# Own-part products of a four-layer graph kernel: six of them made among layer 2's sums, the rest within layer 1

## The chip, the cores and the metric

The kernel runs on one core of one Trainium2 chip. The metric is the device time of one execution in microseconds (us): the median of five runs before the change is 1888.71 us (1886.83 to 1902.47). A change of less than about 0.5% (9.4 us) is about what a measurement of this kernel can't tell from no change.

## What is computed

Four graph layers run one after the other over 3327 nodes with 512 features. Layers 0 and 3 are attention layers; layer 1 takes the mean over all neighbours; layer 2 takes the mean over the first 64 neighbours. Each layer adds its result to its input and normalises the rows. Layer 2 is the one whose parts move, and layer 1 stands just before it:

```
# layer 1
agg = mask @ x / max(deg, 1)
out = relu(concat(x @ W_self + b_self, agg @ W_nb + b_nb) @ W_comb + b_comb)
x = layernorm(x + out)
# layer 2
nb_mean = sum of the first 64 neighbours' rows / max(count, 1)
xj = leaky_relu(nb_mean @ W_nb.T + b_nb)
xi = leaky_relu(x @ W_line.T + b_line)      # the own part
x = layernorm(x + xi + where(count > 0, xj, 0))
```

The own part xi needs a block's rows of x alone and no neighbour. The weights W_nb and W_line have to be transposed on the chip first.

## The kernel before

**Tiling.** The 3327 rows are 26 blocks of 128 (the last has 127). `xres[b]` holds block b's rows in the chip's memory from layer to layer. Each block has a list of its neighbours, cut into chunks of 128 edges; block 0 is dense and takes 26 chunks of whole table rows instead, blocks 1 to 25 have 19 chunks (block 1) down to 5, 201 in all. In layers 1 and 2 a chunk's neighbour rows are gathered from a table in DRAM (`t1_d`, `t2_d`; 1024 fp32 numbers a row, so 512 KB a chunk) by an indirect DMA of POOL (L973), and summed into the block's accumulator by two matmuls with a 0/1 selection matrix `selr` (L1491).

**Ring.** The gathered chunks lie in a ring of buffers (class `Ring`, L576): in layers 1 and 2 one part of 11 slots (`gm`) and one of 4 (`gn`), by the constants `RING` (L544) and `MORE` (L545). A gather waits until the matmuls that read its slot's last content are done. `groups` (L953) cuts a list into groups of at most 4 chunks and never across the end of a part; `first_items` (L1445) gives block 0's chunks in groups of 4, and `take` (L588) skips a part with less room than the group.

**Order of the work.** From L1438 on the order of the instructions is the order in which the code emits them. Generators stand in two lists, `work` and `ends`; `both` (L1499) advances each by one `yield`. `mean_group` (L1460) is a group: gather, selection, matmuls, one step each (layer 2 before has one step more: DVE writes the selection as 8-bit numbers into `sall`, L1476, which layer 3 reads again, and ACT then turns it into `selr`, L1483). When a block's last group is summed, `layer1_end` (L1531) or `layer2_end` (L1640) follows, a step at a time, between the next groups' instructions.

**Layer 1.** `layer1_end` normalises the block, transposes it (four small matmuls, L751, and an ACT copy, L754), multiplies it by W_nb (`wn2`, L1545, four matmuls at L766), adds the bias (DVE, L1548), splits it into two parts (`halves`: an ACT cast at L822, a DVE subtraction at L824) in a tile `t2` with one buffer, and SP stores that to the table `t2_d` (L739). Then block 0's layer-2 sum is made from the same tile (L1561). `self_part` (L1522) makes layer 1's own part for the last 16 blocks with the weights `wx`, one per group, in the first 16 groups.

**Layer 2's own parts.** `own_part` (L1570) multiplies a transposed block by W_line (`wl2`, L1576) and three DVE instructions (L1579 to L1581) add the result to `xres[b]`. For b < 26 - `LATE` = 16 it is started inside `layer1_end` with the transposed block at hand (L1550). The blocks 16 to 25 are put on the list `late`; the loop at L1595 starts them one per step once layer 1's groups are all emitted, each with transposes of its own:

```
        while late or work.live or ends.live:
            if late and not work.live:
                ends.add(own_part(late.pop(0)))
            both()
```

Layer 2's groups are emitted after this loop, so on PE all ten late own parts stand ahead of layer 2's first matmul.

**Layer 2 needs all of layer 1.** Its first gather on POOL waits until the last `t2` has landed in `t2_d`. The blocks come in the order of `mixed` (L1450): 1, 25, 24, 23, 22, 2, 21, 20, 19, 18, 3 and so on; block 1 is big, the blocks from 15 on have 5 or 6 chunks. `score_parts` (L1613) prepares layer 3's weights at the start of layer 2.

**Weights.** `transposed_weights` (L1406) loads and transposes both W_nb and W_line near the end of layer 0, through one buffer.

**After layer 2** POOL clears the ring for layer 3 (L1670, two memsets: 11616 and 4096 columns), `finish` (L1021) makes a few table-wide numbers, and layer 3 begins: its ring has 22 slots and 3 (of 520 columns), and four further pieces of the same 4096 columns hold the rows of its dense block 0 (`first_block`, L1099).

Of the kernel before, what the change touches and what calls it, by code (L numbers as in the profile page):

```python
# [536 lines left out]
LATE = 10  # L537
# [7 lines left out]
MORE = 4096  # L545
# [77 lines left out]
def sparse_path(ctx, tc, flag_i, x, adj, l0_w, l0_a1, l0_a2, l1_w_self, l1_b_self, l1_w_nb, l1_b_nb,  # L623
# [366 lines left out]
    class Gat:  # L990
# [108 lines left out]
        def first_block(self, pool, ps, pacc, mp, none, done, room):  # L1099
# [4 lines left out]
            for h in range(H):  # L1104
# [10 lines left out]
            held = [t.rearrange("p (h m) -> p h m", m=M) for t in  # L1115
                    (room[:, q * H * M:(q + 1) * H * M] for q in range(GROUP))]
            G = held[-1]
# [7 lines left out]
            def unit(c):  # L1125
                m = LAST if c == NB - 1 else P
                G = held[c % GROUP]
# [139 lines left out]
    wx = pool_in(wxlay, "l1wx", side="right").tile([P, DC, D], F32, name="wx")  # L1267
# [138 lines left out]
    def transposed_weights():  # L1406

        for src, o in ((l2_w_nb, wn2), (l2_w_line, wl2)):
            for k in range(DC):
                raw = fin.tile([P, D], F32, name="raw", tag="tb")  # L1410
                nc.sync.dma_start(raw, src[k * P:(k + 1) * P, :])
                yield
                yield
                pt = ps.tile([P, DC, P], F32, name="pt", tag="tr")
                for c in range(DC):
                    nc.tensor.transpose(pt[:, c, :], raw[:, c * P:(c + 1) * P], ident)
                nc.scalar.copy(o[:, :, k * P:(k + 1) * P], pt)

    w2lay = ExitStack()
    for k, item in enumerate(groups(pools[0], order)):  # L1420
# [5 lines left out]
        if ready == NB - 1 and wn2 is None:  # L1426
            listlay.close()
            aside = pool_in(ctx, "s_more")
            sp = pool_in(ctx, "s_sel", 3)
            wp = pool_in(w2lay, "l2w")  # L1430
            wn2 = wp.tile([P, DC, D], F32, name="wn2")
            wl2 = wp.tile([P, DC, D], F32, name="wl2")
            work.add(transposed_weights())
# [26 lines left out]
    def mean_group(item, table, whole0, done, sall=None):  # L1460
# [11 lines left out]
        else:  # L1472
            G = gather(ring, table, l, c0, g)
            yield
            if sall is not None:
                have = select(sp, l.dst, c0, g, BF16, kept(sall, b, at, g))  # L1476
                yield
            S = sp.tile([P, GROUP, P], F32R, name="selr")
            if sall is None:
                nc.vector.tensor_tensor(S[:, :g], lane1[:, None, :].to_broadcast([P, g, P]),  # L1480
                                        l.dst[:, c0:c0 + g, None].to_broadcast([P, g, P]), ALU.is_equal)
            else:
                nc.scalar.activation(S[:, :g], have, AF.Identity)  # L1483
# [18 lines left out]

    ring = Ring(2 * D, room.tile([P, RING], F32R, name="gm", tag="ring").bitcast(F32),
# [3 lines left out]
    left0 = [0]  # L1507


    with ExitStack() as lay:  # L1510
# [5 lines left out]
        nc.sync.dma_start(bl, row(l2_b_line, D))  # L1516
        ps = pool_in(lay, "l1ps", 2, space=PSUM)
        xts = pool_in(lay, "l1xt", 3)
        acc0 = pool_in(lay, "l1p0", space=PSUM).tile([P, D], F32, name="acc0")
        early, late = list(range(NB - LATE0, NB)), []  # L1520
# [10 lines left out]
        def layer1_end(b, acc):  # L1531
# [38 lines left out]
        def own_part(b, xt=None):  # L1570

            yield
            if xt is None:
                xt = transposed(xts, ps, xres[b])
                yield
            po = times(ps, xt, wl2)  # L1576
            yield
            xi = fin.tile([P, D], F32, name="xi")
            nc.vector.tensor_add(xi, po, bl)  # L1579
            nc.vector.scalar_tensor_tensor(xi, xi, SAGE_ALPHA, xi, ALU.mult, ALU.max)  # L1580
            nc.vector.tensor_add(xres[b], xi, xres[b])  # L1581

        for items in (first_items(), groups(ring, range(1, NB))):
            for item in items:
# [15 lines left out]
    wxlay.close()  # L1600
# [3 lines left out]
    with ExitStack() as lay:  # L1604
        fin = pool_in(lay, "l2f", 2)
        ps4 = pool_in(lay, "l2p4", 4, space=PSUM)
        ps = Banks(pool_in(lay, "l2p2", 2, space=PSUM), po=ps4)

        wp = pool_in(lay, "l3w")
# [30 lines left out]
        def layer2_end(b, acc):  # L1640
            yield
            y = xres[0]
# [16 lines left out]
        for item in groups(ring, mixed()):  # L1659
            work.add(mean_group(item, t2_d, None, lambda b, acc: ends.add(layer2_end(b, acc)), sall))  # L1660
# [10 lines left out]
        g3.finish(fin, ps)  # L1671
    mlay.close()


    with ExitStack() as lay:
        pools = (Ring(H3 * (OUT3 + 2), rows, extra[:, :MORE - GROUP * H3 * (OUT3 + 2)]), pool_in(lay, "l3s", 3),
# [13 lines left out]
        def verdict():  # L1690
# [11 lines left out]
            for ls in lists:  # L1702
                for l in ls:
# [16 lines left out]
                               nl, layer3, extra[:, MORE - GROUP * H3 * (OUT3 + 2):])  # L1720
# [61 lines left out]
```

## Time and profile before

| | |
|---|---|
| median of 5 runs | 1888.71 us (1886.83, 1886.95, 1888.71, 1896.29, 1902.47) |
| the profiled execution | 1884.82 us, its span 1882.9 us |
| mean granted TensorE clock | 0.914 |
| layer 1's sums (first to last matmul of L1491) | 717.9 to 1104.1 us |
| layer 2's sums | 1172.0 to 1458.0 us |
| layer 3's first sums of block 0 | from 1498.7 us |
| PE, DVE, ACT, POOL busy | 82%, 65%, 42%, 48% of the span |

How to read it: PE does the matmuls, DVE and ACT work on tiles, POOL issues the gathers, SP the plain loads and stores. A line of the timeline has a start, a duration, an engine, a line of the kernel, what it writes <- reads and, in brackets, how long the engine was idle before and what ended that. A line of the table by stretch has for each engine its busy time and (x) its instructions, then the granted clock of PE, the busy share of the 16 DMA engines and what they moved in GB/s. At a DMA share of about 1.00 or a little above the DMA engines have no free time.

### The profile page before, as it was taken

Reading aid. Unit: us, or ns where it says so; the run is one execution under the profiler, and the core shown is the slowest. Engines: PE = TensorE matmul, PEld = TensorE weight load, DVE = VectorE, ACT = ScalarE, POOL = GpSimd, SP = SyncE. Lnnn points to the kernel's source line nnn. Section 1 sums busy time; section 2 is a strip of 40 time slices with the busy share of each in tenths; the row PEclk is TensorE's granted clock in tenths of the full one; section 3 lists DMA queues with packets and bytes.
Section 4 is the critical chain, followed back from the end, with each engine's and each line's share of the span. In section 5 each row is a group of like instructions: output and inputs, shape, how many; then the busy total and the mean of one; then the engine's idle time right before and its main releaser. Section 6 shows DMA issues by size and latency. Waiting matters only on the chain.

```text
span 1882.9 us, 24596 instructions
## 1 busy us (share of the span) xinstructions
PE 1541.0 (82%) x7493; PEld 1052.8 (56%) x7493; DVE 1228.2 (65%) x3217; ACT 783.7 (42%) x2465; POOL 900.2 (48%) x984
## 2 busy tenths in 40 slices
PE   5898767888999998998899987769777657877775
PEld 4665545665666664554455543457556445656654
DVE  7999857787887862134677764534344566766786
ACT  5557834555755753210111121234233212545564
POOL 1000265455655522546656613766665433666660
PEclk9899879999999999999899999798898778998897
DMA  8624776776766538999999944999999264666661
GB/s 293 207 82 135 265 223 205 239 242 199 256 213 195 175 107 320 369 332 388 360 365 379 377 152 180 342 362 338 373 370 335 93 194 116 190 192 189 194 191 47
DMA packets 146178, 460.50 MB, mean 245 GB/s; under 512 B 24357, under 2 KB 25893, under 8 KB 146038
## 3 DMA queue, kind: packets, MB, share of 16 engines
q0 software_dynamic: 93776, 329.72, 53.2%
q1 hardware_dynamic: 52262, 129.14, 19.5%
q8 instruction: 61, 1.00, 0.2%
q14 instruction: 79, 0.65, 0.1%
HBM read 403.93 MB, written 54.85 MB: 244 GB/s over the span
## 4 chain that ended last, share of the span: by engine, by line
PE 48%; DVE 19%; issue 10%; DMA 8%; ACT 6%; another core or an unknown queue 5%; POOL 3%; SPq 1%; DVEq 0%; ACTq 0%; POOLq 0%
PE po L766 16%; PE acc L1205 14%; PE acc L1491 7%; PE po L1005 5%; DMA gm<-t_d,idx 4%; DVE cand L884 3%; PE pt L751 2%; POOL gm L973 2%; PE pg L1177 1%; DVE cand L898 1%; DVE sl L896 1%; DMA gx<-t_d 1%; DVE gr L1197 1%; DVE gt L1197 1%
## 5 line engine op out<-in xcount | busy, mean ns | idle before, releaser
L973 POOL DMA_INDIRECT gt<-t_d,idx x243 | 239.5, 986 | 394.6 <-DVE some L900 216.3
L973 POOL DMA_INDIRECT gm<-t_d,idx x300 | 302.1, 1007 | 229.6 <-PE acc L1491 65.6
L1205 PE MATMUL acc<-gt,sel 128*128 128x264 f32 (+2 forms) x972 | 245.0, 399 | 1.9 <-issue 1.9
L973 POOL DMA_INDIRECT gr<-t_d,idx x177 | 170.7, 965 | 153.4 <-issue 47.5
L1205 PE MATMUL acc<-gr,sel 128*128 128x260 f32 (+2 forms) x708 | 195.9, 427 | 34.0 <-issue 27.4
L766 PE MATMUL po<-wn,xt 128*128 128x512 f32 x416 | 205.5, 640 | 14.9 <-ACT xt L754 7.1
L1491 PE MATMUL acc<-gm,selr 128*128 128x512 f32 (+3 forms) x636 | 197.5, 442 | 21.3 <-DMA gm<-t_d,idx 13.2
L1205 PEld LDWEIGHTS acc<-gt,sel 128*128 128x128 f32 (+2 forms) x972 | 182.8, 195 | 51.6 <-issue 24.9
L1205 PEld LDWEIGHTS acc<-gr,sel 128*128 128x128 f32 (+2 forms) x708 | 142.3, 209 | 68.1 <-issue 38.9
L1491 PEld LDWEIGHTS acc<-gm,selr 128*128 128x128 f32 (+3 forms) x636 | 117.0, 196 | 73.6 <-DMA gm<-t_d,idx 24.1
L1005 PE MATMUL po<-w,xt 128*128 128x262 f32 x416 | 115.7, 439 | 46.5 <-issue 29.4
L1197 DVE TENSOR_TENSOR gt<-gt,pg 128x1536 f32<-128x1536 f32 (+3 forms) x75 | 140.6, 1875 | 16.0 <-ACT sel L1192 13.8
L766 PEld LDWEIGHTS po<-wn,xt 128*128 128x128 f32 x416 | 81.7, 204 | 108.6 <-issue 89.9
L1005 PEld LDWEIGHTS po<-w,xt 128*128 128x128 f32 x416 | 89.0, 219 | 73.0 <-issue 34.9
L973 POOL DMA_INDIRECT gn<-t_d,idx x102 | 102.6, 1006 | 54.7 <-issue 22.1
L884 DVE MAX8 cand<-val 128x8 f32<-128x832 uint16 (+38 forms) x259 | 125.4, 524 | 0.0
L751 PE MATMUL pt<-s_ident,xres 128*128 128x128 f32 x520 | 83.0, 285 | 43.0 <-DMA xres<-in_x_dram 18.0
L1005 PE MATMUL po<-gt,xt 128*128 128x268 f32 x416 | 107.9, 405 | 2.6 <-ACT xt L758 1.3
L1165 ACT ACTIVATE far<-place,nmid 128x384 int16<-128x384 int16 (+3 forms) x139 | 87.8, 634 | 49.4 <-issue 25.2
L751 PEld LDWEIGHTS pt<-s_ident,xres 128*128 128x128 f32 x520 | 64.4, 146 | 72.5 <-issue 44.4
L754 ACT COPY xt<-pt 128x512 f32<-128x512 f32 x86 | 50.6, 588 | 128.6 <-PE pt L751 70.1
L1197 DVE TENSOR_TENSOR gr<-gr,pg 128x1536 f32<-128x1536 f32 (+3 forms) x56 | 101.8, 1817 | 2.7 <-ACT gr L1190 2.3
(283 smaller groups left out, 2848.3 us busy)
## 6 DMA issues: line engine op xcount, KB each, us to landing
t_d<-t SPq DMA_DIRECT2D x50, 512.0 KB
ab<-in_adj_dram SPq DMA_DIRECT2D x25, 832.0 KB
ab<-in_adj_dram SPq DMA_DIRECT2D x25, 831.5 KB
gm<-t_d POOLq DMA_DIRECT2D x17, 512.0 KB
t_d<-tg SPq DMA_DIRECT2D x25, 264.0 KB
t_d<-tg SPq DMA_DIRECT2D x25, 260.0 KB
gx<-t_d SPq DMA_DIRECT2D x25, 260.0 KB
xres<-in_x_dram SPq DMA_DIRECT2D x25, 256.0 KB
```

What stands on the lines that cost most here:

```text
L751: nc.tensor.transpose(pt[:, c, :], src[:, c * P:(c + 1) * P], ident)
L754: nc.scalar.copy(xt, pt)
L766: nc.tensor.matmul(po, xt[:, c, :], w[:, c], start=c == 0, stop=c == DC - 1)
L884: nc.vector.max(out=top, in_=seg)
L896: nc.vector.max(out=top, in_=cf)
L898: nc.vector.match_replace(out=cf, in_to_replace=top, in_values=cf, imm_value=0.0)
L973: nc.gpsimd.indirect_dma_start(out=t[:m, c, :], out_offset=None, in_=table[:, :], in_offset=bass.IndirectOffsetOnAxis(ap=l.idx[:m, c0 + c: ...
L1005: nc.tensor.matmul(pw[s], xt[:, c, :], self.w[:, c, s, :], start=c == 0, stop=c == DC - 1)
L1165: nc.scalar.activation(far[:, :g * P], place[:, c0 * P:(c0 + g) * P], AF.Abs, bias=l.nmid, scale=2.0)
L1197: nc.vector.tensor_mul(Gc[:, :, :OUT], Gc[:, :, :OUT], w[:, :g].rearrange("p c (h o) -> p (c h) o", o=1).to_broadcast([P, g * H, OUT]))
L1205: nc.tensor.matmul(accs[b][s], S[:m, c, :], G[:m, c, s * hh * M:(s + 1) * hh * M], start=at + c == 0, stop=at + c == chunks_of[b] - 1)
L1491: nc.tensor.matmul(accs[b], S[:m, c, :], G[:m, c, k * D:(k + 1) * D].bitcast(F32R), start=at + c + k == 0, stop=k == 1 and at + c == n - 1)
```

## The change

- The six blocks `LATER` = 1, 2, 3, 23, 24, 25 get their own part in layer 2: it is started together with the block's first group. All other blocks get it inside `layer1_end`, if `wl2` exists by then, and at the end of layer 1 otherwise (that is block 0 alone).
- W_line is loaded and transposed in layer 1, after the last `self_part`, into the room of `wx`, which is no longer needed then. Layer 0 transposes W_nb alone, through two buffers.
- `t2` gets two buffers in layer 1 (one before), the transposed blocks four (three before).
- The ring's second part shrinks from 4096 to 2600 columns: 2 slots in layers 1 and 2 (4 before), 5 slots in layer 3 (3 before). Layer 3's dense block gets four tiles `gd` of its own.
- In layer 2 DVE writes the selection straight into `selr`, and ACT copies it to `sall` behind it; `mean_group` has one step less there, and `selr` two buffers (three before).
- `tg`, the tile that layer 2 stores for layer 3, has one buffer (two before).

The instruction streams that come of it: layer 1 has 73 groups for blocks 1 to 25 (63 before), layer 2 has 76 (65), layer 3 has 62 (64). Up to layer 1's last sum 18 own parts are made (16 before), of blocks 4 to 21.

```diff
-LATE = 10
+LATER = (1, 2, 3, 23, 24, 25)
-MORE = 4096
+MORE = 5 * 520
...
-            tb = pool.tile([P, H, self.M], F32, name="tg")
+            tb = pool.tile([P, H, self.M], F32, name="tg", bufs=2 - self.k)
...
+            S = sp.tile([P, GROUP, P], F32R, name="selr")
+            nc.vector.tensor_tensor(S[:, :g], lane1[:, None, :].to_broadcast([P, g, P]),
+                                    l.dst[:, c0:c0 + g, None].to_broadcast([P, g, P]), ALU.is_equal)
             if sall is not None:
-                have = select(sp, l.dst, c0, g, BF16, kept(sall, b, at, g))
-                yield
-            S = sp.tile([P, GROUP, P], F32R, name="selr")
-            if sall is None:
-                nc.vector.tensor_tensor(S[:, :g], ..., ALU.is_equal)
-            else:
-                nc.scalar.activation(S[:, :g], have, AF.Identity)
+                nc.scalar.activation(kept(sall, b, at, g), S[:, :g].bitcast(F32), AF.Identity, saturate=False)
...
-            t2 = fin.tile([P, 2, D], F32R, name="t2", bufs=1)
-            if b < NB - LATE:
-                ends.add(own_part(b, xt))
+            t2 = fin.tile([P, 2, D], F32R, name="t2")
+            if b in LATER or wl2 is None:
+                late.append(b)
             else:
-                late.append(b)
+                ends.add(own_part(b, fin, xts, bl, xt))
...
                 if early:
-                    ends.add(self_part(early.pop(0)))
+                    parts.append(self_part(early.pop(0)))
+                    ends.add(parts[-1])
+                elif wl2 is None and not any(map(parts.__contains__, ends.live)):
+                    wl2 = wxroom.tile([P, DC, D], F32, name="wl2", tag="wx")
+                    ends.add(transposed_weights(l2_w_line, wl2, wp))
                 both()
-        while late or work.live or ends.live:
-            if late and not work.live:
-                ends.add(own_part(late.pop(0)))
+        now = [b for b in late if b not in LATER]
+        while now or work.live or ends.live:
+            if now and not work.live:
+                ends.add(own_part(now.pop(0), fin, xts, bl))
             both()
...
         for item in groups(ring, mixed()):
+            if item[4] == 0 and item[0] in LATER:
+                ends.add(own_part(item[0], fin, fin, bias1))
             work.add(mean_group(item, t2_d, None, lambda b, acc: ends.add(layer2_end(b, acc)), sall))
```

More of the change, by code (lines that the diff above doesn't have):

```diff
@@ L1404, in sparse_path, with transposed_weights @@
     wn2 = None
[L1406 to L1411, printed above, removed]
-                yield
[L1413 to L1417, printed above, removed]
+    def transposed_weights(src, o, pool):
+        for k in range(DC):
+            raw = pool.tile([P, D], F32, name="raw")
+            nc.sync.dma_start(raw, src[k * P:(k + 1) * P, :])
+            yield
+            yield
+            pt = ps.tile([P, DC, P], F32, name="pt", tag="tr")
+            for c in range(DC):
+                nc.tensor.transpose(pt[:, c, :], raw[:, c * P:(c + 1) * P], ident)
+            nc.scalar.copy(o[:, :, k * P:(k + 1) * P], pt)
     w2lay = ExitStack()
@@ L1501, in both, with own_part @@
         ends.step()
+    def own_part(b, fin, xts, bl, xt=None):
+        yield
+        if xt is None:
+            xt = transposed(xts, ps, xres[b])
+            yield
+        po = times(ps, xt, wl2)
+        yield
+        xi = fin.tile([P, D], F32, name="xi", bufs=1)
+        nc.vector.tensor_add(xi, po, bl)
+        nc.vector.scalar_tensor_tensor(xi, xi, SAGE_ALPHA, xi, ALU.mult, ALU.max)
+        nc.vector.tensor_add(xres[b], xi, xres[b])
+        owned.add(b)
     ring = Ring(2 * D, room.tile([P, RING], F32R, name="gm", tag="ring").bitcast(F32),
```

48 lines of the change are left out of this document (17 added, 31 removed).

## The prediction

> **What bounds the kernel now.** I read the table by stretch first, for the busy share of the DMA engines from layer 1 to layer 2 (its last columns are granted clock, DMA share, GB/s):
>
> ```profile
> core 0: us, PE busy (x) PEld busy (x) DVE busy (x) ACT busy (x) POOL busy (x), PEclk, DMA share, GB/s
> 800.00:820.00 20.00, 20.00 (x66) 10.77 (x65) 5.48 (x9) 4.07 (x9) 10.40 (x12) 1.00 1.03 393
> 820.00:840.00 20.00, 20.00 (x65) 10.82 (x64) 4.80 (x11) 2.90 (x6) 9.64 (x10) 1.00 0.88 322
> 1040.00:1060.00 20.00, 20.00 (x63) 10.73 (x63) 15.09 (x33) 3.21 (x8) 11.67 (x12) 1.00 1.01 366
> 1100.00:1105.00 5.00, 5.00 (x21) 3.26 (x21) 3.94 (x7) 1.40 (x4) 0.00 (x0) 1.00 0.01 4
> ...
> 1145.00:1150.00 5.00, 3.59 (x13) 1.68 (x11) 2.08 (x3) 0.58 (x1) 3.78 (x5) 1.00 1.03 413
> 1155.00:1160.00 5.00, 4.27 (x11) 1.86 (x9) 1.19 (x2) 0.58 (x1) 0.00 (x0) 0.70 0.00 1
> 1160.00:1165.00 5.00, 4.27 (x13) 2.07 (x14) 2.21 (x4) 0.58 (x1) 0.00 (x0) 1.00 0.00 0
> 1165.00:1170.00 5.00, 3.47 (x8) 1.21 (x7) 2.17 (x5) 0.00 (x0) 0.00 (x0) 1.00 0.00 0
> 1170.00:1175.00 5.00, 3.03 (x7) 2.45 (x8) 5.00 (x16) 2.23 (x5) 1.54 (x1) 0.66 0.00 0
> 1325.00:1350.00 25.00, 18.53 (x77) 14.91 (x78) 7.31 (x20) 8.67 (x41) 15.92 (x16) 0.86 1.02 364
> ```
>
> In both layers' sums the DMA engines are full (1.01 to 1.03); in layer 1 PE is full beside them (20.00 of 20), in layer 2 it has a quarter free (18.53 of 25). Between the layers DMA stands still twice: about 1100, while layer 1's last blocks are finished, and from 1155 to 1175. POOL's timeline tells why:
>
> ```profile
> 1089.54 1.38 POOL L973 DMA_INDIRECT gm<-t_d,idx  x1 [0.30 <-PE acc L1491]
> 1132.48 0.97 POOL L973 DMA_INDIRECT gm<-t_d,idx  x1 [41.57 <-DMA t_d<-t]
> ...
> 1149.56 0.94 POOL L973 DMA_INDIRECT gm<-t_d,idx  x1 [0.30 <-issue]
> 1173.46 3.04 POOL L973 DMA_INDIRECT gm<-t_d,idx  x1 [22.95 <-PE acc L1491]
> ```
>
> Layer 2's gathers start when the last t2 has landed (1132.48), fill the ring by 1150, and then wait 22.95 us for PE to free a slot. PE's timeline shows what it does meanwhile:
>
> ```profile
> 1094.51 6.37 PE L766 MATMUL po<-wn,xt 128*128 128x512 f32 x8 [3.37 <-ACT xt L754]
> ...
> 1118.51 3.60 PE L766 MATMUL po<-wn,xt 128*128 128x512 f32 x8
> 1121.94 3.60 PE L766 MATMUL po<-wl,xt 128*128 128x512 f32 x8
> ...
> 1164.77 3.70 PE L766 MATMUL po<-wl,xt 128*128 128x512 f32 x8 [0.73 <-ACT xt L754]
> 1171.97 5.37 PE L1491 MATMUL acc<-gm,selr 128*128 128x512 f32 x16 [3.50 <-ACT selr L1483]
> ```
>
> Up to 1168.5 PE makes late own parts (po<-wl), though gathered chunks have been there since about 1140. The chain that ended last runs through them from 1118 to 1170. What the change is worth is the DMA time lost there, not PE time saved.
>
> **The parts, one by one.**
>
> 1. *The standstill from 1155 to 1175.* Layer 2's sums ran from the first gather at 1132.5 to the last matmul at 1457.3, 324.8 us, with four stretches of 5 us at share 0.00. If gathers never pause, they need 305 us from the landing of the last t2 on. **-20.**
>
> 2. *Two buffers for t2.* ACT's timeline has, at the end of layer 1:
>
> ```profile
> 1093.35 0.62 ACT L822 CAST t<-tb 128x512 fp32r<-128x512 f32 x1 [7.36 <-DMA t_d<-t]
> ...
> 1126.07 0.59 ACT L754 COPY xt<-pt 128x512 f32<-128x512 f32 x1 [6.51 <-PE pt L751]
> 1126.55 0.62 ACT L822 CAST t<-tb 128x512 fp32r<-128x512 f32 x1
> ```
>
> The cast waited 7.36 us for the last store; the copy xt behind it on ACT waited too, and PE behind that: 3.37 us idle, then a product of 6.37 us instead of 3.70 at a granted clock of 0.51. With a second buffer the cast waits for the store before. 3.37 + 2.67 = **-6**. The other such waits (55.3 us in 9 over layer 1) lie where DMA is full: nothing.
>
> 3. *The last cast.* At 1126.55 it stood behind the copy xt of a late own part, whose transposes stood behind another own product; its input (L1548) was ready at 1122.8. In the new order only block 0's own part is there, and its copy comes before. 3.7 us, and some 0.4 us more on DVE behind L1579 to L1581: **-4**.
>
> 4. *One own product more before the last products of W_nb.* In the new PE order an own product stands ahead of block 24's product too: 3.5 us, of which 1.15 us were idle (1109.72, waiting for ACT). **+2.3.**
>
> 5. *Layer 1's sums.* Blocks 0 to 3 lose their own products (4 x 3.43 = 13.7 us of PE), W_line's 16 transposes come in (4 x 0.60 = 2.4). They lie at about 820 to 920, where DMA is full but for 820 to 860 (0.88 and 0.91): -4 to 0, taken -2. Blocks 16 to 21 get own products: 6 x 3.43 = 20.6 us of PE from about 1050 to the last sum, where PE is 92 to 100% busy. A block of 6 chunks then has some 3.2 us of sums, 0.9 of small matmuls and 6.2 to 6.9 of products, 10.3 to 11 us, against 3.8 MB of DMA, about 10 us at 375 GB/s. So +0.7 each, +4; if PE was the whole bound there, 20.6 less the 5 us that it idled: +15. Taken +7. W_line's four loads of 256 KB move with it; on SP each waits for the transposes of the one before, with stores of t2 and loads of zb queued behind; zb is loaded 3 blocks ahead, so this is hidden unless a load waits longer than a block (10 us). Sum **+5** (-4 to +15).
>
> 6. *A smaller ring in layer 1.* Block 0's groups of four don't fit the part of 2 slots, so 8 slots serve them instead of 12: four chunks (2.1 MB, 5.6 us of DMA) are issued later at the start. Against that PE gets there sooner by a wait for W_line (1.76 us at 731.5) and four sets of transposes. -5 to +6, **0**.
>
> 7. *Six own parts in layer 2.* PE: 6 x (0.60 + 3.70) = 25.8 us, all within the first 92 of 201 chunks. Those take DMA some 92 x 1.5 = 138 us, in which PE was 80% busy: now nearly full. ACT 6 x 0.58, DVE 6 x 2.1 us (DVE at 40%). Hidden if the ring stays ahead; uncovered it is the whole 26. Each `layer2_end` of the six waits for its own part, which is 3 steps old by then. 0 to +26, **+4**: the first groups, where `score_parts` fills DVE too (1180 to 1190: 9.55 of 10 us), are the tight place.
>
> 8. *The selection.* DVE writes selr itself (551 ns in layer 1, L1480) where sall (545, L985) and then selr (538, L1483) stood in line; the sums wait for DMA anyway. Two buffers instead of three let DVE wait for the sums two groups back: -2 to +5, **0**. `tg` with one buffer holds ACT if a store takes over a block's 7 us or more: 0 to +3, **0**.
>
> 9. *The memset.* After layer 2 a DVE instruction of usually 547 ns (L827) takes 11.03 us beside POOL's two memsets, on the chain that ended last:
>
> ```profile
> 1458.16 9.78 POOL L1670 MEMSET gr<- 128x11616 f32 x1 [6.61 <-PE acc L1491]
> 1467.88 3.52 POOL L1670 MEMSET gx<- 128x4096 f32 x1
> ```
>
> ```profile
> 1460.66 11.03 DVE xres L827
> ```
>
> It ends as the second memset does (1471.7 and 1471.4), so the second counts. It shrinks to 2600 columns: 3.52 x 1496/4096 = **-1.3**. The Trainium skill's page "SBUF — State Buffer", section "SBUF: two separate sides", has DVE and GpSimd share one port pair as a lock held for a whole instruction. By that rule DVE could get in between the memsets and part 9 would be 0; the row shows it got in behind both. The same section warns that DVE's 2-port instructions keep GpSimd from writing its DMA descriptors, which speaks against more DVE work beside layer 2's gathers; its section "Who interferes with whom" names copies and tensor_scalar as holders of both ports, and an instruction of two tensors in SBUF only against what GpSimd reads; by it the own parts (L1579 to L1581) cost the gathers nothing.
>
> 10. *Layer 3.* 62 groups instead of 64, 27 ring slots instead of 25: -2 to +2, **0**.
>
> Sum: -20 - 6 - 4 + 2.3 + 5 + 4 - 1.3 = **-20**. The profiled execution, 1884.82 us, becomes 1865. It lies 3.9 us under the median of the five runs; against that median I predict **1869 us**. All low ends together give -42 (1847), all high ends +28 (1917).
>
> **The rivals.**
>
> *PE becomes the bound of layer 2's first half.* The hole closes, but part 7 costs 22 instead of 4: 1869 + 18 = 1887, no change. For it: PE comes to about 100% in those 138 us. Against it: its clock there was 0.80 to 1.00 after waits and rises with fewer of them.
>
> *The smaller ring starves DMA* (slower). Place: layer 2's sums. If the 15 slots and not the DMA engines set the pace, a slot turns round in 15 x 1.48 = 22.2 us (gathers came every 1.48 us from 1250 to 1460), and 13 slots give 1.71 us: 201 x 0.23 = +46. 1869 + 46 = 1915. It decides from the point where a turn-round stays above 13 x 1.48 = 19.2 us. For it: POOL's longer idle times end on freed slots. Against it: the share of 1.00 to 1.02, and only some 17 of 100 us that POOL waits beyond its usual 0.3.
>
> *The hole only moves.* Layer 2's first selections stand on DVE behind the rest of layer 1, and `score_parts` takes some 25 us of DVE; if PE's first sums come more than 18 us after the first gather, the ring is full again and DMA stops for 10 us: 1879.
>
> **How the numbers follow.** The forecast (1850 to 1877, most of the low ends, with part 7 up to 12) 0.62; the hole moves 0.10; PE the bound 0.15; the ring starves DMA 0.13. The range reaches from 1850 to 1895 and leaves out the starved ring, the high ends all at once, and the last 3 us of the low ones. Faster by over 0.5% (below 1879.3): 0.62 and half of 0.10, 0.67; within 0.5%, which is about what a measurement of this kernel can tell from no change: 0.05 + 0.15 = 0.20; slower (above 1898.1) 0.13.
>
> **What would show it.** Right: no stretch of 5 us with DMA share 0.00 after layer 2's first gather, POOL's 22.95 us gone, layer 2's last sum some 305 to 310 us after the first gather, which starts near 1128; no cast waiting for a store of t2; L827 after the last sum near 9.7 us. Wrong: a DMA share under 0.95 in layer 2's sums (the ring), PE full there with POOL waiting (PE), layer 1's last sum after 1110 (part 5).

## The result, and the profile after

The changed kernel takes 1889.59 us (median of 36 runs, 1872.43 to 1900.28) beside 1888.50 us of the kernel before (62 runs): ratio 1.0004, 95% interval 0.999 to 1.0018. The forecast gain of 20 us did not come; nothing measurable changed. The profiled execution takes 1887.61 us, its span 1885.9.

By stage, in us, from POOL's and PE's timelines (layer 1: its first gather to its last sum; tail: to layer 2's first gather; layer 2: its first gather to its last sum; middle: to layer 3's first sum of block 0):

| | layer 1 | tail | layer 2 | middle | layer 3 |
|---|---|---|---|---|---|
| before | 391.0 | 28.4 | 325.6 | 40.6 | 384.2 |
| after | 398.8 | 25.8 | 322.9 | 38.6 | 388.3 |

Layer 2, which was to lose 16 us, lost 2.7. The table by stretch of the changed kernel, with the stretches shown of before and those in which DMA now stands still (last columns: granted clock, DMA share, GB/s):

```profile
720.00:730.00 10.00, 7.56 (x21) 3.27 (x21) 1.39 (x2) 2.81 (x5) 1.19 (x3) 1.00 0.90 310
730.00:740.00 10.00, 4.59 (x11) 2.98 (x10) 0.69 (x1) 2.22 (x4) 1.27 (x3) 0.83 0.59 146
...
1060.00:1080.00 20.00, 20.00 (x65) 10.93 (x64) 15.03 (x33) 3.43 (x8) 10.65 (x11) 1.00 0.93 347
1100.00:1105.00 5.00, 5.00 (x16) 2.82 (x16) 4.72 (x13) 0.49 (x2) 0.00 (x0) 1.00 0.45 128
...
1160.00:1165.00 5.00, 0.00 (x0) 0.00 (x0) 0.00 (x0) 0.00 (x0) 2.33 (x4) 0.50 1.04 307
...
1195.00:1200.00 5.00, 5.00 (x18) 2.75 (x17) 1.53 (x3) 0.18 (x2) 0.86 (x1) 0.77 0.06 25
1200.00:1205.00 5.00, 5.00 (x25) 4.29 (x24) 4.61 (x12) 2.81 (x18) 1.08 (x1) 1.00 0.48 131
1205.00:1210.00 5.00, 5.00 (x28) 4.25 (x27) 0.36 (x1) 1.58 (x6) 0.95 (x1) 1.00 0.00 0
...
1325.00:1350.00 25.00, 19.84 (x69) 15.24 (x70) 9.93 (x26) 8.81 (x37) 15.79 (x17) 0.80 1.02 373
```

The standstill of 1155 to 1175 is gone: there the share is 0.99 to 1.04. Added up over stretches of 5 us it had cost 24 us of DMA time from 1150 to 1185. From 1195 to 1230 a new one costs 18, most of it (16) in four stretches in which PE is full (5.00 of 5: the three shown and the one from 1220). POOL's timeline has the same in its waits:

```profile
1136.04 0.97 POOL L973 DMA_INDIRECT gn<-t_d,idx  x1 [38.48 <-DMA bias<-in_L_gnn_b_line_dram]
...
1199.10 0.86 POOL L973 DMA_INDIRECT gn<-t_d,idx  x1 [7.57 <-PE acc L1482]
```

The wait of 22.95 us has gone; three of 7 us (from 1190.6 on) stand in its place, each for PE to free a slot. What PE does there:

```profile
1142.31 1.19 PE L1482 MATMUL acc<-gn,selr 128*128 128x512 f32 x2 [8.45 <-DMA gn<-t_d,idx]
...
1179.45 5.78 PE L766 MATMUL po<-wl,xt 128*128 128x512 f32 x8 [0.83 <-issue]
...
1192.06 6.30 PE L766 MATMUL po<-wl,xt 128*128 128x512 f32 x8 [4.28 <-ACT xt L754]
...
1200.47 7.23 PE L1005 MATMUL po<-w,xt 128*128 128x262 f32 x32
...
1209.81 3.60 PE L766 MATMUL po<-wl,xt 128*128 128x512 f32 x8
...
1217.67 5.49 PE L1005 MATMUL po<-w,xt 128*128 128x262 f32 x16 [3.33 <-ACT xt L760]
```

The first sums come at 1142 and not at 1172. Then the own products (po<-wl) meet the layer-3 products of the blocks that end early (po<-w), two of the own products at a mean granted clock of 0.63 and 0.58: 5.78 and 6.30 us for what takes 3.60 at 1209.81 (1.00 there). Ahead of the first PE had stood still for 7.34 us (to 1166.38), and the clock was still 0.50 up to 1180; ahead of the second for 4.28 us. The Trainium skill's page "TensorE: Matmul & The Clock Gate", section "HAM oscillation — how this bites in real kernels", warns of just this, half the clock after a pause of some 3.4 us; the 4.28 us ahead of the 6.30 agree.

ACT's timeline at three places: layer 1's first selection, the last cast of layer 1, and the stretch of the new standstill:

```profile
735.89 0.63 ACT L1466 ACTIVATE selr<-row 128x512 fp32r<-128x512 fp8e4 x1 [4.10 <-DMA t_d<-t]
...
1130.53 0.62 ACT L822 CAST t<-tb 128x512 fp32r<-128x512 f32 x1 [6.78 <-issue]
...
1215.73 0.38 ACT L1016 COPY tg<-po 128x260 f32<-128x260 f32 x1 [5.93 <-DMA t_d<-tg]
```

No cast waits for a store of t2 any more, and the last one follows 0.8 us after its product (1126.12 to 1129.72), not 4.4. But layer 1's first selection waits for a store of layer 0's last tile: `selr` now lies in room that layer 0 leaves, so the first sum comes 25 us after the first gather (4.8 before). And `tg` with one buffer makes ACT wait. The memsets after layer 2, and the DVE instruction beside them (L827) on the chain that ended last:

```profile
1459.07 9.78 POOL L1672 MEMSET gr<- 128x11616 f32 x1 [7.17 <-PE acc L1482]
1468.79 2.27 POOL L1672 MEMSET gx<- 128x2600 f32 x1
```

```profile
1462.40 8.95 DVE xres L827
```

It ends at 1471.3 again with the second memset (1471.1). By the lock of the Trainium skill's page "SBUF — State Buffer", section "SBUF: two separate sides", it could have got in between the two; the measurement decides against that here too.

### The profile page after: what moved, and what is told of

Same layout as the page of the kernel before. It is cut to its first block, busy times and chain, and to the rows that moved or that the text cites. A ratio compares the mean times of both kernels' runs of the same rounds, so it can differ in the third digit from the quotient of the medians.

```text
span 1885.9 us, 24566 instructions
## 1 busy us (share of the span) xinstructions
PE 1541.6 (82%) x7481; PEld 1058.8 (56%) x7481; DVE 1227.4 (65%) x3230; ACT 787.2 (42%) x2465; POOL 901.7 (48%) x984
## 4 chain that ended last, share of the span: by engine, by line
PE 60%; DVE 15%; issue 10%; DMA 6%; ACT 5%; another core or an unknown queue 2%; POOL 1%; SPq 0%; DVEq 0%; ACTq 0%; POOLq 0%
PE po L766 18%; PE acc L1203 18%; PE acc L1482 9%; PE po L1005 6%; PE pt L751 2%; PE pg L1175 2%; DMA gm<-t_d,idx 2%; DVE cand L884 2%; DMA raw<-in_L_gnn_W_line_dram 1%; PE acc L1141 1%; DVE cand L898 1%; DMA gd<-t_d 1%; DVE gt L1195 1%; DVE sl L896 1%
## 5 line engine op out<-in xcount | busy, mean ns | idle before, releaser
L973 POOL DMA_INDIRECT gm<-t_d,idx x342 | 345.5, 1010 | 204.8 <-PE acc L1482 84.7
L1482 PE MATMUL acc<-gm,selr 128*128 128x512 f32 (+2 forms) x736 | 228.2, 444 | 35.6 <-issue 12.4
L1203 PE MATMUL acc<-gt,sel 128*128 128x264 f32 (+2 forms) x972 | 251.5, 407 | 0.0
L1203 PE MATMUL acc<-gr,sel 128*128 128x260 f32 (+3 forms) x684 | 186.8, 424 | 29.3 <-issue 23.2
L766 PE MATMUL po<-wn,xt 128*128 128x512 f32 x416 | 195.2, 613 | 12.9 <-ACT vc L938 5.6
L1482 PEld LDWEIGHTS acc<-gm,selr 128*128 128x128 f32 (+2 forms) x736 | 137.4, 197 | 94.8 <-issue 40.3
L1471 DVE TENSOR_TENSOR selr<-lane,dst 128x384 fp32r<-128x384 bf16 (+3 forms) x149 | 74.2, 506 | 159.8 <-PE acc L1482 86.2
L1203 PEld LDWEIGHTS acc<-gr,sel 128*128 128x128 f32 (+3 forms) x684 | 136.6, 208 | 62.7 <-issue 35.3
L1175 PEld LDWEIGHTS <-ds 128*128 128x128 bf16 x1332 | 57.7, 99 | 87.8 <-issue 60.8
L766 PE MATMUL po<-wl,xt 128*128 128x512 f32 x208 | 100.0, 626 | 5.1 <-ACT xt L754 4.3
```

The source lines that it names most:

```text
L766: nc.tensor.matmul(po, xt[:, c, :], w[:, c], start=c == 0, stop=c == DC - 1)
L973: nc.gpsimd.indirect_dma_start(out=t[:m, c, :], out_offset=None, in_=table[:, :], in_offset=bass.IndirectOffsetOnAxis(ap=l.idx[:m, c0 + c: ...
L1175: nc.tensor.matmul(pe[:, c], ds[:, c * P:(c + 1) * P], self.own[:, k, :, b], start=k == 0, stop=k == 2)
L1203: nc.tensor.matmul(accs[b][s], S[:m, c, :], G[:m, c, s * hh * M:(s + 1) * hh * M], start=at + c == 0, stop=at + c == chunks_of[b] - 1)
L1482: nc.tensor.matmul(accs[b], S[:m, c, :], G[:m, c, k * D:(k + 1) * D].bitcast(F32R), start=at + c + k == 0, stop=k == 1 and at + c == n - 1)
```

## The experiments

My theory after this: the hole closed, and its gain was given back in two places, by layer 1, which grew 7.8 us, and by own products that hold back the sums in layer 2's first third. Rivals: the ring of 13 slots; `score_parts` on DVE; waits that nothing explains. Of the last there were many: in the first profiles PE, DVE and ACT stood for 150 to 248 us each in waits put down to "issue" or to a releaser that the trace lacks, before and after alike; for instance

```profile
DVE selr L1471 <- remote: 49.7, 8, 10.5
```

(us in all, times, longest), of the changed kernel. The experiments ran on three chips on each of which the kernel before takes 1752 to 1753 us (the record does not say on which chip the first runs were made), and these waits are 0 to 34 us an engine in the two kernels' profiles there. Their stages are compared with each other only. All ratios are to the kernel before on the same chip.

| | layer 1 | tail | layer 2 | ratio (95%) |
|---|---|---|---|---|
| before_2 | 384.8 | 28.6 | 315.2 | 1.0004 (0.9991 to 1.0018) |
| after_2 | 402.5 | 25.8 | 303.4 | 0.999 (0.9973 to 1.0007) |
| no_own | 401.1 | 25.8 | 293.6 | 0.9935 (0.9914 to 0.9957) |
| spread | 401.7 | 25.8 | 296.1 | 0.9924 (0.9904 to 0.9945) |
| no_prep | 399.5 | 26.0 | 301.6 | 1.0013 (0.9995 to 1.0031) |
| tg_room | 396.1 | 25.9 | 302.5 | 0.9981 (0.997 to 0.9991) |
| before_ring13 | 386.0 | 28.6 | 315.4 | 1.0029 (1.0014 to 1.0045) |
| sel_room | 396.2 | 25.8 | 308.9 | 0.9987 (0.9973 to 1.0001) |
| start13 | 401.7 | 26.5 | 299.9 | 0.9986 (0.997 to 1.0001) |
| t2_one | 393.4 | 26.0 | 310.8 | 0.9984 (0.9966 to 1.0002) |
| own9 | 391.7 | 23.8 | 301.0 | 0.9924 (0.9897 to 0.9951) |
| own13 | 386.8 | 23.8 | 305.8 | 0.9905 (0.9882 to 0.9928) |
| best1 | 399.3 | 25.8 | 292.4 | 0.9905 (0.9891 to 0.9919) |
| best3_13 | 392.5 | 23.7 | 297.9 | 0.9892 (0.9874 to 0.991) |
| best4 | 404.2 | 26.5 | 293.8 | 0.9946 (0.9927 to 0.9965) |
| best5 | 400.6 | 25.0 | 301.0 | 0.9967 (0.9949 to 0.9985) |

The stages are those of one execution each. after_2, no_own, spread, tg_room and no_prep have the same layer 1, and it took 396.1 to 402.5 us: a difference of some 6 us between two lines says nothing by itself. Layer 2 scatters more: with the six own parts in their place it took 299.9 to 310.8 us (after_2, no_prep, tg_room, sel_room, start13, t2_one).

**The two kernels again.**

> The changed kernel itself once more, as the base beside the experiments: in their runs both kernels were some 7% shorter than in the first ones (the kernel before 1753 us), since many waits of PE, DVE and ACT that nothing in the profile explains are gone. Theory 'given back': the standstill after the first third of a layer 2 that now has no such waits is still there, layer 2 takes 306 to 312 us from first gather to last sum, and the ratio to the kernel before stays within 0.997 to 1.003. Rival 'unexplained waits': without them the change pays what was forecast, about 0.989.

> The kernel before the change once more, for its profile beside the others. Layer 1 takes 385 to 388 us from its first gather to its last sum, layer 2 takes 312 to 317 us from first gather to last sum (with 15 slots as with 13), and its standstill between the layers is as in the first profile: about 35 us from the first gather to the first sum. Ratio 1.000.

Without the unexplained waits the change still pays nothing, so they are not the cause. The stages are now plain: tail -2.8, layer 2 -11.8, middle -2.7 (40.3 and 37.6), layer 3 the same, and layer 1 **+17.7**. The table by stretch for layer 1 as a whole, of the kernel before and of the changed one:

```profile
657.60:1042.40 384.80, 360.55 (x1159) 201.53 (x1159) 199.30 (x412) 69.25 (x155) 218.72 (x230) 0.98 0.99 365
```

```profile
657.40:1059.90 402.50, 371.58 (x1175) 210.29 (x1176) 203.22 (x427) 71.66 (x157) 214.36 (x230) 0.95 0.96 350
```

PE is busy 94% of the first and has 11 us more to do in the second; DMA falls from 0.99 to 0.96. Where the time goes shows when layer 1 is cut at its 200th gather. Up to there it took 327.7 and 333.6 us (332.0 and 329.9 in the first profiles), and PE did less in the changed kernel, 302.6 us and not 309.3. From there to the last sum, of the kernel before, the changed one and own13 (told below), which leaves the late own parts to layer 2:

```profile
985.30:1042.40 57.10, 51.22 (x171) 27.81 (x169) 42.46 (x93) 10.69 (x27) 28.83 (x29) 1.00 0.93 348
```

```profile
991.00:1059.90 68.90, 68.90 (x221) 38.21 (x220) 53.60 (x112) 11.02 (x26) 29.38 (x29) 1.00 0.82 298
```

```profile
986.40:1043.20 56.80, 49.71 (x168) 27.56 (x167) 42.95 (x94) 10.65 (x26) 28.64 (x29) 1.00 0.99 363
```

In the changed kernel PE never pauses there (68.90 of 68.90) and DMA falls to 0.82: PE has 17.7 us more to do, 5.9 of them fit into its idle time, and the stretch is 11.8 us longer. In the first profiles it is 59.0 and 68.9 us, 9.9 longer. The own products taken away before the 200th gather bring nothing that stands out of the scatter.

**What the own parts cost in layer 2.** no_own leaves out the six; spread moves their blocks back in the order:

```diff
-            if item[4] == 0 and item[0] in LATER:
-                ends.add(own_part(item[0], fin, fin, bias1))
```

```diff
+    def spread_out():
+        rest, later = [b for b in mixed() if b not in LATER], list(LATER)
+        for i, b in enumerate(rest):
+            yield b
+            if i > 2 and i % 2 and later:
+                yield later.pop(0 if i % 4 == 3 else -1)
...
-        for item in groups(ring, mixed()):
+        for item in groups(ring, spread_out()):
```

> The changed kernel with the six own parts of layer 2 left out (blocks 1, 2, 3, 23, 24, 25 then lack that term; nothing else differs). Theory 'given back': the standstill between the layers did close, and what it gave is lost again at 1195 to 1230 us, where own products, queued on PE behind copies that ACT and DVE make late beside layer 3's weight preparation, hold back the sums. Then without them layer 2 takes 305 to 310 us from its first gather to its last sum (323 with them, 325 before the change), and the time falls by 13 to 18 us, to 1872 to 1877. Rival 'ring': 13 slots instead of 15 are too few whatever stands on PE; then layer 2 still takes 318 to 325 us, with stretches at DMA share 0.00, and the time falls by no more than 5 us.

> The changed kernel, with the six blocks whose own part is made in layer 2 moved later in layer 2's order of blocks: the first is fifth, then every third, so that all six are begun between about 1170 and 1330 us, most of them behind layer 3's weight preparation. Theory 'given back': PE has a quarter of its time free there, so the own parts are hidden, no stretch of 5 us stands at DMA share 0.00, layer 2 takes 305 to 312 us and the time falls by 10 to 18 us, to 1872 to 1880. Rival 'PE bound wherever they stand': 26 us of PE are not hidden anywhere; layer 2 stays at 318 to 325 us and the time at 1885 to 1892. Rival 'ring': the same 318 to 325.

Both as the theory has it: by these pairs of executions the six cost 9.8 us in their place and 2.5 when moved, and the time falls by 0.65% and 0.76% against the kernel before. With the six moved layer 2 took 292.4 to 296.1 us in three executions (spread, best1, best4), all of them under the 299.9 to 310.8 with the six in place. (The numbers of us expected for layer 2 were those of the slower first runs.) DMA tells the same: added up over stretches of 5 us it lost 21 us in layer 2 of before_2, 10.7 in after_2, 2.5 in no_own and 1.1 in spread. The same stretch after layer 2's start, first of the changed kernel (after_2), then of spread:

```profile
1141.00:1146.00 5.00, 5.00 (x25) 4.23 (x24) 2.09 (x9) 0.82 (x2) 0.00 (x0) 1.00 0.51 156
1146.00:1151.00 5.00, 5.00 (x22) 3.24 (x21) 0.56 (x1) 1.58 (x6) 2.84 (x3) 1.00 0.33 75
1151.00:1156.00 5.00, 1.96 (x7) 0.97 (x6) 2.08 (x3) 2.14 (x14) 1.97 (x2) 1.00 1.00 373
1156.00:1161.00 5.00, 5.00 (x17) 3.97 (x16) 3.76 (x10) 1.81 (x6) 0.00 (x0) 0.66 0.52 186
1161.00:1166.00 5.00, 5.00 (x24) 3.77 (x23) 3.14 (x8) 2.97 (x16) 3.06 (x4) 1.00 0.55 165
```

```profile
1136.00:1141.00 5.00, 5.00 (x25) 4.28 (x24) 1.48 (x5) 1.62 (x6) 3.88 (x4) 1.00 1.05 401
1141.00:1146.00 5.00, 4.42 (x22) 3.35 (x20) 1.17 (x2) 0.00 (x0) 2.95 (x4) 1.00 1.02 251
1146.00:1151.00 5.00, 2.20 (x5) 1.80 (x6) 0.09 (x1) 2.75 (x14) 1.86 (x2) 0.73 1.06 392
1151.00:1156.00 5.00, 5.00 (x20) 3.59 (x19) 0.00 (x0) 0.00 (x0) 0.94 (x1) 0.93 0.92 270
1156.00:1161.00 5.00, 4.38 (x17) 2.77 (x16) 3.68 (x8) 2.50 (x8) 3.92 (x4) 1.00 0.87 279
```

The standstill is gone with the own products moved, and each of the six takes 3.60 us there; in after_2 the first three take 4.18, 4.04 and 5.40. Why they cost time in the first third: no_prep leaves out DVE's score columns for layer 3 and puts small fills with zero in their place, tg_room gives `tg` a second buffer.

```diff
-            score_weights(w3, wp, a3, H3, OUT3)
+            for c in range(DC):
+                score = w3[:, c].rearrange("p s (h m) -> p s h m", h=H3 // 2)
+                for k in (0, OUT3 + 1, OUT3 + 2):
+                    nc.vector.memset(score[:, :, :, k], 0.0)
```

```diff
+            self.turn = getattr(self, "turn", 0) + self.k
+            if self.turn % 2:
+                spare = near0.rearrange("p b n -> p (b n)")[:, :4 * H * self.M].bitcast(F32)
+                tb = spare.rearrange("p (h m) -> p h m", h=H)
+            else:
+                tb = pool.tile([P, H, self.M], F32, name="tg", bufs=2 - self.k)
```

> The changed kernel with the making of layer 3's score columns on DVE left out: twelve small fills with zero stand in place of the 20 instructions of score_weights (layer 3 then weights all neighbours alike; nothing else differs). In the changed kernel these stand on DVE in one piece of 12 us between the first layer-2 blocks' instructions, and the own product after them waits 3.8 us on PE for an ACT copy that waits for DVE's moments. Theory 'queue behind the preparation': without it layer 2 takes 294 to 298 us (303 with it, 294 without own parts) and the time falls by 5 to 9 us, ratio 0.994 to 0.996. Rival 'PE time': the own products and the first blocks' products for layer 3 fill PE by themselves; layer 2 stays at 301 to 304 us and the ratio at 0.998 to 1.000.

> The changed kernel, with a second buffer for tg in layer 2 (every other tile lies in the room of near0, which is no longer needed then); nothing else differs. In the changed kernel ACT waits 5 to 6 us for the store of tg in the stretch where DMA stands still, and PE 3 us behind it. Theory 'given back, tg in it': the waits of the copies for a store vanish, layer 2 becomes 3 to 6 us shorter and the time falls by as much. Rival 'PE order alone': the wait is covered, and the time the same within 2 us.

My theory of the queue behind the preparation fell: without it layer 2 takes 301.6 us, as the rival had it, and PE still waits as long for the copy; PE's timeline of no_prep:

```profile
1126.69 5.40 PE L766 MATMUL po<-wl,xt 128*128 128x512 f32 x8 [3.63 <-ACT xt L754]
```

ACT has two square roots ahead of that copy, and these wait for DVE's moments of a block (L789). With the preparation gone the moments stand on DVE behind the three instructions of the own part before, and the first of those waits for its product on PE (1116.73 to 1120.58):

```profile
1120.62 0.69 DVE L1503 TENSOR_TENSOR xi<-po,bias 128x512 f32<-128x512 f32 x1 [3.14 <-PE po L766]
```

So the own parts and the ends of the blocks hold each other up in turn. The wait for tg's store is worth 0.9 us in layer 2, less than the scatter; its time isn't told apart from the changed kernel's.

**The ring, and layer 1's start.** before_ring13 cuts the old kernel's ring to 13 slots, sel_room gives `selr` a room of its own, start13 adds to that all 13 slots for block 0:

```diff
-                aside.tile([P, MORE], F32R, name="gn", tag="aside").bitcast(F32))
+                aside.tile([P, MORE], F32R, name="gn", tag="aside").bitcast(F32)[:, :4 * D])
```

```diff
             aside = pool_in(ctx, "s_more")
+            sp = pool_in(ctx, "s_sel", 2)
...
-        sp = pool_in(lay, "l1s", 3)
...
-        sp = pool_in(lay, "l2s", 2)
```

```diff
-        for c0 in range(0, NB, GROUP):
-            yield 0, None, c0, min(GROUP, NB - c0), c0
+        c0 = 0
+        while c0 < NB:
+            g = min(GROUP, NB - c0, ring.ahead())
+            yield 0, None, c0, g, c0
+            c0 += g
```

> The kernel before the change, with the ring's second part cut to 2 slots in layers 1 and 2 (13 in all) and nothing else altered. Theory 'given back': the ring costs layer 2 next to nothing; layer 2 stays within 4 us of 325 from first gather to last sum. Layer 1's first 26 chunks have 8 slots instead of 12, which costs its start 0 to 5 us; time within 0 to +6 us of the kernel before. Rival 'ring': layer 2 is 10 us longer or more (up to 46), and the time with it: 1898 or above.

> The changed kernel, with the selection tiles selr (two of them) given a room of their own before layer 0 ends, as before the change, instead of room that layer 0's tiles leave. In the changed kernel layer 1's first sum came at 736.6 us instead of 717.9, ACT's first selr waiting for a store of layer 0's last tile, and POOL then waited 16.9 us for a slot. Theory 'room': with a room of its own the first selr comes at about 712 and the first sum by 722; DMA has no stretch under 0.90 from 720 to 750; layer 1's last sum comes 4 to 7 us earlier than 1110, and the time falls by 3 to 7 us. Rival 'slots': the 8 slots that block 0 has instead of 12 hold back the start; then the DMA share from 730 to 740 stays near 0.6 and the time is the same.

> The changed kernel with selr in a room of its own and with block 0's chunks in layer 1 cut by what the ring has left (groups of 4, 4, 3, 2 and so on), so that all 13 slots serve them and not 8. Theory 'slots at the start': POOL's wait of 22 us for PE in the first 25 chunks shrinks to 10 or less, the 50th gather comes at 82 to 85 us after the first (88.6 with the room alone, 82.8 before the change), and layer 1 is 3 to 6 us shorter from first gather to last sum than with the room alone: 391 to 394; ratio 0.995 to 0.997. Rival 'taken back': PE is full later in layer 1, so the earlier start only makes later gathers wait; layer 1 stays at 396 to 400, ratio 0.998.

The ring rival falls: layer 2 takes 315.4 us with 13 slots and 315.2 with 15. In layer 1 the 50th gather behind the first comes 6.8 us later (89.6 us after it instead of 82.8), of which 1.2 are left at the end; in POOL's timeline of before_ring13 it is this wait:

```profile
690.05 2.09 POOL L1468 DMA_DIRECT2D gm<-t_d  x4 [21.83 <-PE acc L1491]
```

The room does bring the first sum back to 4.8 us after the first gather, but the second group's still comes 33 us after it, as before the change (690.9 and 690.6 us), since the next copy waits for layer 0's stores too: next to nothing is won (0.9987). start13 loads more at once (20th gather behind the first at 38.2 us instead of 45.7) and is late by the 50th (92.6 and 88.6): taken back, as the rival said. Why it is behind, and best4 with it, I have not found out; its groups are cut differently from there on.

**Two buffers for t2.** t2_one goes back to one (`bufs=1`).

> The changed kernel with one buffer for t2 in layer 1 again (two after the change). The prediction put the second buffer at 6 us. If that holds, layer 1 takes 5 to 7 us longer from first gather to last sum (402 becomes 407 to 409) or its tail does, and the ratio is 1.002 to 1.004. Rival: where PE is full, the wait for the store was covered by the products that stand around it, and the second buffer is worth 0 to 2 us: ratio 0.999 to 1.001.

ACT's waits for that store are back (40.1 us in 10), and nothing is lost. The rival holds, for the changed kernel, in which PE is full at layer 1's end; the second buffer alone in the kernel before was not tried.

**Layer 1's late own parts.** own9 and own13 have the three repairs of best1 (told below), with orders of blocks of their own, and more own parts in layer 2: those of blocks 20 to 22 and of 16 to 22. best3_13 has best1's order and starts those of 20 to 22 at layer 2's beginning (the first cut is own13's, the second best3_13's):

```diff
-LATER = (1, 2, 3, 23, 24, 25)
+LATER = (1, 2, 3, 16, 17, 18, 19, 20, 21, 22, 23, 24, 25)
...
+        head = [b for b in mixed() if b not in LATER][:4]
+        yield from head
+        yield from (b for b in mixed() if b not in head)
```

```diff
+            if item[4] == 0 and item[0] == start:
+                for b in PUT:
+                    ends.add(own_part(b, fin, fin, bias1))
+                start = None
```

> The changed kernel with the three repairs (order, room for selr, second buffer for tg) and three more own parts in layer 2: those of blocks 20, 21 and 22, whose blocks, too, then come after five others without an own part. Theory 'late own parts hold layer 1': its last blocks lose the products that PE had no room for; from the 180th gather on layer 1 is 4 to 6 us shorter (399 becomes 393 to 396 from first gather to last sum), the tail 5 to 7 us shorter (25.8 becomes 19 to 21), and layer 2 3 us longer or less; ratio 0.983 to 0.987. Rival 'layer 2 full': nine own parts, 39 us of PE, no longer fit beside the sums; layer 2 is 8 to 13 us longer and the ratio stays at 0.990.

> As own9, with all of blocks 16 to 25 and 1 to 3 getting their own part in layer 2, behind four blocks without one: thirteen own parts, 56 us of PE in a layer 2 of about 292 us in which PE was busy some 80% with six. Theory 'late own parts hold layer 1': layer 1 takes 386 to 389 us from first gather to last sum as before the change with 13 slots, the tail 19 to 21 us, layer 2 295 to 303 us; ratio 0.979 to 0.985. Rival 'layer 2 full': layer 2 is 12 us longer or more, 305 and above; ratio 0.986 to 0.992.

> The kernel with three repairs (order, room for selr, second buffer for tg), and three more own parts in layer 2, those of blocks 20, 21 and 22, which are all started together with layer 2's first group, where PE stands idle for some 8 us before the first chunk has landed. Theory 'idle PE is free, busy PE is not': these three cost layer 2 only 0 to 4 us (292 to 297 us; own9, which put them among the sums, took 301), while layer 1 keeps own9's 392; ratio 0.985 to 0.988. Rival 'they hold back the first sums': 13 to 16 us of own products at a clock of 0.5 stand ahead of the first sum, the 13 slots fill up, and DMA stops: layer 2 is 300 us or more and the ratio 0.990 to 0.992.

Layer 1 came as expected: 386.8 us without the own parts of blocks 16 to 22, 12.5 less than best1 and about what the kernel before has with 13 slots (386.0). From the 200th gather to the last sum it takes 56.8 us, as before the change (57.1 and, with 13 slots, 56.6); with three of the seven left out 61.1 to 64.5 (own9, best3_13, best5), with all seven in 65.3 to 68.9 in ten executions. So the late own parts are what made layer 1's end longer. But layer 2 takes it all back, 13.4 us more than best1 for seven more; how much of that is their number and how much the other order was not separated. Layer 2 as a whole, of best1 and of own13:

```profile
1081.00:1373.40 292.40, 256.95 (x939) 177.82 (x940) 140.23 (x333) 102.06 (x416) 199.37 (x201) 0.86 1.02 369
```

```profile
1067.00:1372.80 305.80, 270.53 (x1023) 186.60 (x1024) 151.89 (x353) 104.87 (x422) 201.12 (x201) 0.89 0.99 353
```

PE is busy 13.6 us longer, though still idle for 35 us, and DMA drops under 1.00. That idle time does not take up seven more own parts as they stand here: it lies in 33 pieces, in which PE mostly waits for a chunk (20 us); the longest, 9.68 us, the profile puts down to DVE. (The tail, 23.8 us, was expected at 19 to 21.) best3_13 uses the idle piece ahead of layer 2's first sum, and is no faster than best1 as far as the intervals tell.

**Together.** best1 is spread, sel_room and tg_room at once; best4 and best5 add start13's slots to best1 and to best3_13.

> The changed kernel with three repairs at once: the six blocks with their own part in layer 2 moved later in its order, selr in a room of its own, a second buffer for tg. Theory: the gains add; 14 us from the order, 3 to 5 from the room, 0 to 3 from tg, that is a ratio of 0.988 to 0.991 to the kernel before. Rival: with the order changed, the stretch in which tg's store was waited for is gone, and the room's gain is taken back later in layer 1, where PE is full: 0.992 as with the order alone.

> The three repairs (order, room for selr, second buffer for tg) with all 13 slots for block 0's chunks in layer 1. Theory 'slots at the start': 3 to 6 us less than the three repairs alone, ratio 0.987 to 0.989 (0.9905 without). Rival 'taken back': 0.990 to 0.991.

> Everything together: order, room, tg, all 13 slots for block 0, and the own parts of blocks 20 to 22 at the very start of layer 2. If both 'slots at the start' and 'idle PE is free' hold: ratio 0.981 to 0.985. If one of them: 0.985 to 0.988. If neither: 0.990 to 0.992.

best1 beats both kernels by about 1%; what it has over spread lies within the intervals. best4 and best5 differ from best1 and best3_13 by start13's cut of block 0's chunks alone and lose by it, though start13 itself lost nothing (0.9986, beside 0.9987 of sel_room).

## Why the prediction was wrong

By its own parts, with the first profiles and, behind the semicolon, before_2 and after_2:

- **1, the standstill** (-20): closed where it stood, first sum 6.3 us after the first gather; without the own parts layer 2 is 21.6 us shorter than in before_2 (no_own). Right. With part 7, layer 2 was put at -16 and came to -2.7; -11.8. (The 324.8 us there end at the start of the last matmul; to its end it is 325.6.)
- **7, six own parts in layer 2** (+4, bounds 0 and 26): 9.8 us by no_own. This size was off. The first groups were indeed the tight place, but taking DVE's preparation away does not help (no_prep). PE is full where DMA falls (after_2, 1141 to 1151). Own products at a lower clock make 2.8 of the 9.8 us in after_2, and PE stands still for 3.80 us ahead of the third; how the rest divides is not shown.
- **5, layer 1's sums** (+5, of which late blocks +7): this is the step that failed most by before_2 and after_2. With parts 2 and 6, layer 1 was put at -1 and came to +7.8; +17.7 (11 to 18 in five executions). I took the late blocks as half hidden by DMA, with +0.7 a block. From the 200th gather on PE was the whole bound instead (68.9 of 68.9 us busy), and together with part 2 that stretch grew by 9.9; 11.8, where -6 and +7 had been forecast. What came in there counts in full but for the idle time that PE had left: 17.7 - 5.9. The working had this case, as its +15, and did not take it; and the 92 to 100% that it gives for PE there is 91% over 1050 to 1104, with 5.1 us idle, of which part 2 had already counted 3.37 as its own gain. own13 gives 12.5 us back by taking the late own parts out. The early blocks' -2 did not show.
- **2, two buffers for t2** (-6): 0 by t2_one, in the changed kernel. The waits went, but the idle time that they left on PE was taken by the late own parts, and was no gain.
- **6, the smaller ring** (0, bounds -5 and +6): about 6 us at the start, 1 at layer 1's end (before_ring13); as a whole a ratio of 1.0029.
- **3 and 4, the tail** (-1.7): -2.6; -2.8. Right.
- **9, the memset** (-1.3): the memset is 1.25 us shorter and DVE's instruction still ends with it. Right; the middle as a whole -2.0; -2.7.
- **8 and 10**: 0.9 us for tg by tg_room, within the scatter; layer 3 +4.1; +0.1. Right in size. That `selr` would lie in room that layer 0 frees late was not seen; it cost the first sum 20 us and, by sel_room, next to nothing at the end.

Of the rivals, "PE becomes the bound" came nearest, at 1887 us: it had the engine right and the second place, layer 1, not in it; that its number fits so well is luck. "The smaller ring" fell. "The hole only moves" had the outcome, but by DVE, and no_prep, without the preparation, has the same hole.

Open: what the unexplained waits of the first profiles are, and how far they shifted the stages there. In those profiles layer 2 is the larger miss (13.3 us, beside 8.8 in layer 1), and part 7's size explains under half of it; these are single executions.

## What to carry over

When two engines are both near full, closing a hole in one by moving work of the other gives back what the work costs at its new place: count the moved engine time in full, less the idle time that the engine has left in that very stretch (17.7 - 5.9 us at layer 1's end). An average share ("a quarter free") does not show where there is room: the same six own parts cost 9.8 us with five of them in layer 2's first third and 2.5 when spread over the layer. And in a change that moves pools, ask for each tile whose room it gets and when that is free.

## What the runs showed of the hardware

- Both kernels took 7% less in the experiments' runs than in the first ones (1753 and 1889 us), with the same durations of many instructions and packets (the median 4096-byte packet of a gather 0.16 us in both). The waits of PE, DVE and ACT without a recorded cause came to some 550 us in the first profiles of both kernels and to 51 and 59 us in before_2 and after_2. That they make the difference was not shown.
- An own product of 3.60 us took up to 6.44 us after PE had been idle for 3.80 us (t2_one; granted clock 0.50 from 1125 to 1130).
- 13 slots of 512 KB keep DMA as full as 15: layer 2 takes 315.4 and 315.2 us in the kernel before, and best1's DMA share over layer 2 is 1.02 with 13.
- A DVE instruction of 0.55 us (L827) that starts beside two memsets of POOL ends with the second: 11.03 and 8.95 us in the first profiles, 11.02 and 9.72 in before_2 and after_2. Those just ahead of it on DVE were not held up: L1648 takes its usual 0.69 us beside the first memset (1459.62 in the changed kernel).
